# A transformer block on one core: the depthwise conv on TensorE in nine rounds instead of twelve, the Gram matrix in two column strips, and 79 instead of 71 bands convolved on TensorE

## The chip, the cores and the metric

One core of one Trainium2 chip runs the whole kernel. Its engines each work through their own queue in order: TensorE (matrix products), VectorE, ScalarE, GpSimd, and SyncE, which only issues DMAs. The metric is the device time in microseconds.

## The reference

The input x is 16 images of 128 channels, 96 x 96 pixels, f32. Cut to what matters:

```python
xn1 = layernorm(x over channels)
q, k, v = xn1 @ wq.T, xn1 @ wk.T, xn1 @ wv.T            # 8 heads of 16 channels
attn = softmax(l2norm(q) @ l2norm(k).T / 4)             # 16 x 16 per head, sums over all 9216 pixels
x = x + (attn @ v) @ wp.T
xn2 = layernorm(x over channels)
h1 = w_in @ xn2                                         # 128 -> 512 channels
h2 = depthwise 3x3 conv of h1, zero padding
x = x + w_out @ gelu(h2)                                # 512 -> 128 channels
```

## The kernel before

**What is tiled.** An image is worked on in 6 bands of 16 rows, so there are 96 bands (g from 0 to 95). The 512 hidden channels are four chunks of 128. A pair (band, chunk) that is convolved by VectorE is a "job". Pixels come in tiles of 128 (transposed to pixels x channels for the layer norm), four tiles to a call.

**First layer norm and attention.** Per four tiles: four transposes (`forth`, L716), statistics on VectorE (L723), a scaling by ScalarE (`scaled`, L759) into a buffer zT of four 128 x 128 tiles with a column of ones behind each, and a Gram product (`gram`, L768): per tile one product of the tile with itself and the column of ones, 129 columns, added up in one PSUM bank over the 72 tiles of an image. With the Gram matrix and the column sums, `attention` works out a 128 x 128 matrix per image in a chain of small steps; `mix` (L665) applies it. Transposes back to channels (`back`, L802) follow each norm, and ScalarE copies them (`place`, L805) into a ring of normalized rows, xn.

**The hidden layer on VectorE (`conv_job`).** `hidden` (L976): TensorE makes the 18 rows of h1 that a band and its halo need (or 16, with two rows copied over), ScalarE adds the bias (`kept`, L979). Of the nine taps, VectorE does six, one whole-band multiply-add each (`tap`, L1006); ScalarE scales two more (`product`, L999), which GpSimd's DMAs add (L1013); the weights are scaled such that the centre tap is one. `gelu` is L1017.

**The hidden layer on TensorE (`by_matmuls`).** Chunk 3 of some bands is not a job. `split` (L1083): for each of four groups k of 32 channels, four products of 128 x 32 put the left and right half rows and the even and odd rows into four strips of 32 partitions; so partitions 0 to 63 hold the left half (even rows, odd rows) and 64 to 127 the right half. The columns outside the image, and rows outside it, are filled with minus the bias by small products (L1085). ScalarE copies each group (`packed`, L1092). `conv`, called once for the even and once for the odd output rows (y): six taps t (two row offsets of the pair, three columns), two halves c, four groups k: 48 products, each 64 partitions (both row parities) by 32 channels, 384 columns. With 64 x 32 tiles, eight products (2 halves x 4 groups) lie side by side in the array; six such rounds make a call, twelve a band. A pair of row offsets covers four rows where three are needed; the fourth has weight zero. Two GELUs per call read the result (L1113).

**Output.** `ffn_out` (L1139) multiplies with w_out, ScalarE copies it out (`evicted`, L1149), a DMA adds it to the output.

**PSUM.** Two banks for the transposes `tr`, one for `bk`, one for the Gram matrix, and four "h" banks shared by hidden, split, conv, mix and out. A conv call holds two of them until its GELUs have read them.

**Which bands.** `by_pe(g)`: in the first image those in PE_FIRST, in the last those in PE_LAST, else a share PE_SHARE, 3 of 4: 71 bands. Where the kind of band changes to VectorE's, GpSimd sets the padding of chunk 3's buffer to zero (`around`).

**Order.** Each piece of work is entered in a plan with its engine, an estimated duration and a place (its due time, counted in jobs, plus the offset that the table AT holds for its kind). `Plan.order` simulates the engines with these durations: whenever an engine is free it starts the ready piece with the smallest place, if its buffers are free. The order of starts is the order of each engine's queue.

Of the kernel before, what the change touches and what calls it, by code (L numbers as in the profile page):

```python
# [18 lines left out]
BR = 16  # L19
# [3 lines left out]
PE_SHARE = [3, 4]  # L23
PE_LAST = [0, 1, 3, 4]
# [15 lines left out]
    load_1=-318.45, load_2=250.75, tables=-176.75, weights=-199.9, zeros=280.85, pads=489.4, pads_0=-50.0,  # L40
    load_a=-397.35, forth_a=-242.55, stats_a=-48.4, variance_a=52.55, power_a=346.4, scaled_a=65.85,
    gram=-109.85, back_a=-291.7, place_a=163.65, attention=-399.95, mix=-263.75, residual=-1.05, mixed=-9.75,
    add_x=163.65, forth_b=-248.0, stats_b=-54.25, variance_b=-72.2, power_b=-242.45, shift_b=-65.25,
    scaled_b=519.65, back_b=-664.1, place_b=430.4, evicted=-175.6, add_out=-299.05, halo=332.2, hidden=-67.95,
    kept=-6.5, products=623.75, add_last=230.4, tap=-40.35, add_first=521.3, gelu=615.7, split=-72.5,
    packed=65.05, conv=-64.0, conv_gelu=-632.25, out=-63.65, add=699.15, store=57.0, mix_0=-629.3,
    residual_0=-0.45, mixed_0=1.1, add_x_0=-191.4, gram_0=425.2, forth_a_0=-164.1, forth_b_0=-555.1,
    stats_a_0=-203.2, stats_b_0=31.65, scaled_a_0=166.35, scaled_b_0=435.1, back_a_0=198.1, back_b_0=63.05,
    place_a_0=213.65, place_b_0=-41.2, shift_b_0=-104.65, late=436.35, store_x2=-259.8, store_x2_0=-280.3,
    variance_a_0=296.05, variance_b_0=-572.0, power_a_0=446.6, power_b_0=-200.95, attention_0=-700.85,  # L50
    load_a_0=-699.6, hidden_0=-343.05, kept_0=688.75, products_0=-317.3, tap_0=406.55, add_last_0=-476.1,
    add_first_0=-25.55, gelu_0=-695.0, split_0=-310.35, packed_0=-61.1, conv_0=-522.45, conv_gelu_0=2.7,
    out_0=-354.3, evicted_0=38.2,
)
RESERVE = True
Q = 32
STEP = dict(scaled=1.089, hidden=0.115, products=-0.129, tap=-0.536, split=2.985, conv=0.6, out=0.866)
# [191 lines left out]
def tile_restormer_block(  # L249
# [68 lines left out]
    def column(t, v):  # L318
# [5 lines left out]
    whole = const.tile([P, 1], F32, name="whole")  # L324
    nbeta = const.tile([P, P], F32, name="nbeta")
# [20 lines left out]
    SW, SR = W // 2 + 2, BR // 2 + 1  # L346
    PART = SR * SW
    h1s = [
        h1p.tile([P, (BR + 2) * WP + 2 if n != PE_CHUNK else 4 * PART], F32, name=f"h1_{n}") for n in range(NCH)
# [4 lines left out]
    zT_bufs = [h1p.tile([P, QT, P + 1], F32, name=f"zT_{k}") for k in range(ZT_BUFS)]  # L354
# [36 lines left out]

    def at(kind, place, i=1):
        return place + AT[kind if i else kind + "_0"]
# [51 lines left out]
    def packed(k):  # L445
        return strips(h1s[PE_CHUNK][:, k * PART : (k + 1) * PART])

    def zeros(p):

        for t in zT_bufs:  # L450
            pool(300, at("zeros", p - 1), lambda t=t: nc.gpsimd.memset(t[:, :, P:], 1.0), [], [("w", "ones")])
        for t in h1s:
            pool(300, at("zeros", p), lambda t=t: around(t), [], [("w", "pads")])

    def weights(p):
# [8 lines left out]
        def loads_1():  # L464
# [7 lines left out]
            v["col"] = t[:, 10 * P + Q : 10 * P + Q + 24].rearrange("p (a t) -> p a t", a=2)  # L472
            v["by_part"] = t[:, 11 * P : 11 * P + 48]
            v["nb"] = t[:, 11 * P + 48 : 11 * P + 49]
# [78 lines left out]
        def column_of():  # L553
# [6 lines left out]
            nc.vector.tensor_scalar(v["nb"], b, -1.0, None, ALU.mult)  # L560
            nc.vector.tensor_reduce(whole, r, AX.X, ALU.add)
            nc.vector.tensor_scalar(whole, whole, b, None, ALU.mult)
            nc.vector.tensor_scalar(nbeta, ident, v["nb"], None, ALU.mult)
# [85 lines left out]
    def norm(i, second, place_of):  # L649
# [49 lines left out]
        def pixels(s, m):  # L699
# [80 lines left out]
            for h, (q, tr) in enumerate(zip(qs, trs)):  # L780
# [7 lines left out]
                if not second:  # L788
                    pe(QT * 219, at("gram", sh, i), lambda q=q: gram(q), [(*zt, 0), (*zt, 1), ("w", "ones")], [("g", i)])
# [458 lines left out]
```

## Time and profile before

| | before |
|---|---|
| median of 2 runs | 3908.46 us (3906.2 to 3910.72) |
| profiled execution | 3905.63 us, span 3903.9 us |
| granted TensorE clock, mean | 0.996 |
| busy: TensorE, VectorE, ScalarE, GpSimd | 3797.5, 3695.5, 3618.6, 1858.0 us |
| DMA: moved, mean rate | 790.94 MB, 203 GB/s |

How to read the profile: a group's row names the line, the engine, the operation, the tiles, the shape of the TensorE tile (rows*columns), partitions x elements, the count, then busy time and the mean of one in ns, then the idle time before it and what ended that. PE is TensorE's products, PEld its weight loads, DVE VectorE, ACT ScalarE, POOL GpSimd, SP SyncE. A product's length includes the way through the array, so that the lengths of consecutive products overlap; the distance from start to start says what one costs. In the slices each digit is the busy share of one fortieth of the span in tenths.

### The profile page before, as it was taken

How to read it: one execution, taken by the hardware profiler on the slowest of the kernel's cores; microseconds unless marked ns; L12 is line 12 of the kernel's file. 1: busy time of each engine (PE TensorE's matmuls, PEld its weight loads, DVE VectorE, ACT ScalarE, POOL GpSimd, SP SyncE). 2: the span in 40 equal slices, each digit the busy share in tenths (PEclk: the TensorE clock that was granted, in tenths of full speed). 3: DMA queues.
4: the chain of work that ended last, by engine and by line, in shares of the span. 5: the costliest groups of instructions: out<-in, count | busy, mean ns of one | idle time of the engine just before them, and what ended most of it. 6: DMA issues, size and time to landing. Idle time of an engine off the chain costs nothing.

```text
span 3903.9 us, 81207 instructions
## 1 busy us (share of the span) xinstructions
PE 3797.5 (97%) x32452; PEld 2337.7 (60%) x32452; DVE 3695.5 (95%) x3310; ACT 3618.6 (93%) x7473; POOL 1858.0 (48%) x1586
## 2 busy tenths in 40 slices
PE   8899999999999999999999999999999999999998
PEld 6556656566565665656556565665656656666544
DVE  6998999999999999999999999999999999999998
ACT  6899999999999999999999999999999999899995
POOL 4445555354454545545445454544545444454431
PEclk9999999999999999999999999999999999999999
DMA  5899999999999999999999999999999999999997
GB/s 145 174 200 224 193 211 210 200 223 190 218 201 203 221 191 222 196 206 218 186 214 202 208 217 190 224 199 211 216 184 223 203 213 206 195 221 192 205 186 161
DMA packets 188921, 790.94 MB, mean 203 GB/s; under 512 B 21888, under 2 KB 23424, under 8 KB 188544
## 3 DMA queue, kind: packets, MB, share of 16 engines
q0 software_dynamic: 130608, 633.92, 83.7%
q1 hardware_dynamic: 57936, 151.83, 10.8%
q8 instruction: 256, 4.19, 0.4%
q14 instruction: 121, 0.99, 0.1%
HBM read 150.62 MB, written 149.42 MB: 77 GB/s over the span
## 4 chain that ended last, share of the span: by engine, by line
PE 58%; ACT 15%; DMA 10%; DVE 9%; issue 4%; POOL 3%; POOLq 0%; ACTq 0%; DVEq 0%; SPq 0%
PE h L1139 15%; PE h L976 12%; PE h L1105 10%; DMA h<-h 8%; DVE h L1006 8%; PE h L665 4%; PE g L768 4%; ACT h L999 4%; PE h L1083 4%; ACT h L979 3%; ACT zT L759 3%; PE pB_b L802 2%; PE pT_b L716 2%; PE pB_a L802 2%; ACT h L1017 2%
## 5 line engine op out<-in xcount | busy, mean ns | idle before, releaser
L1006 DVE SCALAR_TENSOR_TENSOR h<-h,ratio,h 128x1520 f32<-128x1520 f32 (+1 forms) x1567 | 2750.3, 1779 | 13.7
L1013 POOL DMA_DIRECT2D h<-h x624 | 589.7, 964 | 1045.3 <-ACT h L999 416.6
L1139 PE MATMUL h<-h,woutT 128*128 128x384 f32 x3072 | 1059.6, 489 | 11.1 <-ACT h L979 7.0
L999 ACT ACTIVATE h<-h,ratio 128x1536 f32<-128x1536 f32 (+1 forms) x624 | 1012.4, 1638 | 2.4 <-DMA h<-h 1.3
L976 PE MATMUL h<-xn,winT 128*128 128x384 f32 (+3 forms) x2466 | 947.8, 500 | 31.5 <-ACT h L1149 13.2
L1139 PEld LDWEIGHTS h<-h,woutT 128*128 128x128 f32 x3072 | 570.7, 191 | 389.5 <-issue 21.2
L979 ACT ACTIVATE h<-h,beta 128x384 f32<-128x384 f32 (+1 forms) x1204 | 734.1, 659 | 26.4 <-PE h L976 19.8
L734 POOL TENSOR_TENSOR rstd_a<-ve_a,mhalf 128x4 f32<-128x4 f32 x288 | 545.0, 1895 | 360.3 <-ACT ve_a L730 347.6
L734 POOL TENSOR_TENSOR rstd_b<-ve_b,mhalf 128x4 f32<-128x4 f32 x288 | 528.9, 1841 | 345.6 <-ACT ve_b L730 334.2
L1006 DVE SCALAR_TENSOR_TENSOR h<-h,ratio 128x1536 f32<-128x1536 f32 x313 | 567.0, 1812 | 95.8 <-ACT h L979 94.7
L1105 PE MATMUL h<-h,taps 64*32 64x384 f32 x13632 | 584.7, 484 | 2.3 <-ACT h L979 2.3
L976 PEld LDWEIGHTS h<-xn,winT 128*128 128x128 f32 x2466 | 419.0, 190 | 232.6 <-ACT h L1149 26.6
L1017 ACT ACTIVATE h<-h 128x1536 f32<-128x1536 f32 (+1 forms) x316 | 484.5, 1534 | 32.6 <-DMA h<-h 31.8
L1105 PEld LDWEIGHTS h<-h,taps 64*32 64x32 f32 x13632 | 251.0, 106 | 288.5 <-issue 260.2
L759 ACT ACTIVATE zT<-pT_b,rstd_b 128x128 f32<-128x128 f32 x1132 | 338.0, 440 | 9.3 <-POOL rstd_b L734 8.4
L759 ACT ACTIVATE zT<-pT_a,rstd_a 128x128 f32<-128x128 f32 x1080 | 319.8, 421 | 18.1 <-POOL rstd_a L734 18.0
L768 PE MATMUL g<-zT 128*128 128x129 f32 x2160 | 286.8, 275 | 3.9 <-ACT zT L759 3.9
L665 PE MATMUL h<-xn,mwT 128*128 128x384 f32 x768 | 279.2, 490 | 3.2 <-ACT x L674 2.9
L768 PEld LDWEIGHTS g<-zT 128*128 128x128 f32 x2160 | 263.7, 191 | 6.7 <-ACT zT L759 4.3
L1149 ACT COPY h<-h 128x384 f32<-128x384 f32 x376 | 201.3, 535 | 60.9 <-PE h L1139 60.2
L1083 PE MATMUL h<-xn,winT 128*32 128x441 f32 (+4 forms) x2464 | 250.4, 507 | 1.7 <-ACT h L1113 1.7
L723 DVE BATCH_NORM_STATS2 st_b<-pT_b 128x6 f32<-128x256 f32 x566 | 211.9, 419 | 28.4 <-PE pT_b L716 19.3
(190 smaller groups left out, 3776.3 us busy)
## 6 DMA issues: line engine op xcount, KB each, us to landing
h<-h POOLq DMA_DIRECT2D x520, 768.0 KB, 9.5
h<-h POOLq DMA_DIRECT2D x104, 720.0 KB, 10.5
x<-in_x_dram SPq DMA_DIRECT2D x192, 384.0 KB, 7.5
out_dram<-x SPq DMA_DIRECT2D x190, 384.0 KB, 9.3
x<-in_x_dram POOLq DMA_DIRECT2D x189, 384.0 KB, 9.2
out_dram<-h POOLq DMA_DIRECT2D x94, 768.0 KB, 10.7
out_dram<-x SPq DMA_DIRECT2D x4, 192.0 KB, 1.9
h<-in_L_conv_w_in_dram SPq DMA_DIRECT2D x1, 256.0 KB, 2.7
```

The lines of the kernel that those rows point to most:

```text
L665: nc.tensor.matmul(rows(pm), lhsT=mats[i][0], rhs=interior(i, u), start=True, stop=True)
L734: nc.gpsimd.tensor_tensor(rstd, d["ve"], mhalf, ALU.pow)
L759: nc.scalar.activation(zT(q)[:, k, :P], d["pT", q][:, k, :], AF.Copy, scale=d["rstd"][:, t : t + 1])
L768: nc.tensor.matmul(grams[i][:, : P + 1], lhsT=zt[:, :P], rhs=zt, start=(q == 0 and k == 0), stop=(q == NU * TPU // QT - 1 and k == QT - 1),)
L976: nc.tensor.matmul(rows(ph)[:, k : k + m, :], lhsT=winT[:, n, :], rhs=z, start=True, stop=True)
L979: nc.scalar.activation(window(h1_, r, e - r, 1), rows(d.pop(("ph", r))), AF.Identity, bias=beta[:, n : n + 1])
L999: nc.scalar.activation(d["pr", t][:, o0:o1, :], shifted(t, o0, o1), AF.Copy, scale=ratio[:, n, t : t + 1])
L1006: nc.vector.scalar_tensor_tensor(h3[:, o0:o1, w0:w1], shifted(t, o0, o1, w0, w1), ratio[:, n, t : t + 1], onto, ALU.mult, ALU.add)
L1013: nc.gpsimd.dma_start(out=to[:, o0:o1, :], in_=d["pr", t][:, o0:o1, :], accum_op=ALU.add)
L1017: nc.scalar.activation(h3, h3, AF.Gelu)
L1105: nc.tensor.matmul(halves(d["pc", y, c][k * Q : (k + 1) * Q, :]), lhsT=taps[cs, k, 6 * y + t, :], rhs=packed(k)[cs, up : up + SR - 1, dx : ...
L1139: nc.tensor.matmul(rows(d["po"]), lhsT=woutT[:, n, :], rhs=h3s[g, n][:, s * UR : (s + 1) * UR, :], start=(k == 0), stop=(k == NCH - 1),)
```

## The change

- **Conv.** `conv(y)` is replaced by three steps. `both_rows(y)` does, for output rows of parity y, the three taps of the row pair of which both rows count: 24 products of 64 x 32, three rounds of eight. `single_rows` does the remaining row for both parities at once: for each column tap, half c, parity y and group k one product of 32 partitions (one half, one row parity) by 32 channels, 48 products, three rounds of sixteen 32 x 32 tiles, into all four result banks. The order is both_rows(0), single_rows, both_rows(1); the GELUs of the even rows follow the second step, those of the odd rows the third. Nine rounds instead of twelve, 96 products as before.
- **Packing.** Rows of the packed buffer now lie 50 elements apart with 49 of data; the element between two rows serves as the right neighbour of one and the left neighbour of the next. It is set by GpSimd (`sides`, four small products) whenever the kind of band changes to TensorE's, so the split's side columns are no longer products of each band. The split writes 441 columns per strip; only rows outside the image are still filled with small products.
- **Gram.** Each zT tile has a column of ones on both sides (130 columns). Two tiles k, k+1 are done together as four products of 128 x 64: of one tile, the left 64 channels against 129 columns and the right 64 against 65; of the other the reverse. The two column strips of the array get 194 columns each per pair of tiles. One product of zeros (one partition, 130 columns) opens the accumulation. The Gram matrix so has halves of its off-diagonal blocks in two places; `attention` copies it, transposes it on TensorE, and adds the two with two VectorE adds.
- **Bands.** PE_SHARE is 5 of 6 and PE_LAST has one more: 79 bands.
- **Plan.** Nearly all offsets in AT and STEP have other values, and the estimated durations of the changed pieces are lower (a Gram call 4 x 166 instead of 4 x 219 ns). The tables BY_BAND and BY_BLOCK, new, are empty.

```diff
-PE_SHARE = [3, 4]
-PE_LAST = [0, 1, 3, 4]
+PE_SHARE = [5, 6]
+PE_LAST = [0, 1, 2, 3, 4]
...
-    SW, SR = W // 2 + 2, BR // 2 + 1
-    PART = SR * SW
+    SW, SR = W // 2 + 1, BR // 2 + 1
+    PART = SR * (SW + 1) + 1
...
+    def sides():
+        for k in range(4):
+            nc.gpsimd.tensor_scalar(
+                h1s[PE_CHUNK][:, k * PART : (k + 1) * PART : SW + 1], ones_row[:, : SR + 1], npad[:, k : k + 1], None, ALU.mult
+            )
...
-                for k in range(QT):
-                    zt = zTs[q][:, k, :]
-                    nc.tensor.matmul(
-                        grams[i][:, : P + 1], lhsT=zt[:, :P], rhs=zt,
-                        start=(q == 0 and k == 0), stop=(q == NU * TPU // QT - 1 and k == QT - 1),
-                    )
+                    nc.tensor.matmul(grams[i][:, : P + 2], lhsT=ident[:1, :], rhs=ident[:1, 1:2].to_broadcast([1, P + 2]), start=True, stop=False)
+                done = q == NU * TPU // QT - 1
+                for k in range(0, QT, 2):
+                    for e, half in ((0, 0), (0, 1), (1, 1), (1, 0)):
+                        zt = zTs[q][:, k + e, :]
+                        c0, c1 = (0, P + 1 if e == 0 else P // 2 + 1) if half == 0 else (P // 2 + 1 if e == 0 else 1, P + 2)
+                        hs = slice(half * P // 2, (half + 1) * P // 2)
+                        nc.tensor.matmul(
+                            grams[i][hs, c0:c1], lhsT=zt[:, 1 + half * P // 2 : 1 + (half + 1) * P // 2], rhs=zt[:, c0:c1],
+                            start=False, stop=done and k + e == QT - 1,
+                        )
...
+        @step("PE", 110)
+        def _():
+            nc.tensor.transpose(ps([P, P], "ps_t"), v["gsb"], ident)
+
+        @step("DVE", 380)
+        def _():
+            for own, other in ((low, high), (high, low)):
+                to = v["gsb"][own, other]
+                nc.vector.tensor_add(to, v["ps_t"][own, other], to)
...
-        def conv(y):
-            for c in range(2):
-                d["pc", y, c] = bank((g, "conv", y, c), BR * W // 4)
-            for t in range(6):
-                up, dx = divmod(t, 3)
-                for c in range(2):
-                    cs = slice(c * 2 * Q, (c + 1) * 2 * Q)
-                    for k in range(4):
-                        nc.tensor.matmul(
-                            halves(d["pc", y, c][k * Q : (k + 1) * Q, :]),
-                            lhsT=taps[cs, k, 6 * y + t, :], rhs=packed(k)[cs, up : up + SR - 1, dx : dx + W // 2],
-                            start=(t == 0), stop=(t == 5),
-                        )
+        def product(y, c, k, up, dx, cs, first):
+            nc.tensor.matmul(
+                halves(d["pc", y, c][k * Q : (k + 1) * Q, :]),
+                lhsT=taps[cs, k, 6 * y + 3 * up + dx, :], rhs=packed(k, up, SR - 1, dx + c, W // 2)[cs],
+                start=first and dx == 0, stop=not first and dx == 2,
+            )
+
+        def both_rows(y):
+            if y == 0:
+                banks_of(0)
+            for dx in range(3):
+                for c in range(2):
+                    for k in range(4):
+                        product(y, c, k, y, dx, slice(c * 2 * Q, (c + 1) * 2 * Q), y == 0)
+
+        def single_rows():
+            banks_of(1)
+            for dx in range(3):
+                for c in range(2):
+                    for y in range(2):
+                        for k in range(4):
+                            q = 2 * c + y
+                            product(y, c, k, 1 - y, dx, slice(q * Q, (q + 1) * Q), y == 1)
...
+        steps = ((lambda: both_rows(0), pcs[0]), (single_rows, pcs[0] + pcs[1]), (lambda: both_rows(1), pcs[1]))
+        for z, (work, to) in enumerate(steps):
+            pz = p + STEP["conv"] * z
+            pe(3 * t_mm(UT) + 100, at("conv", pz, g >= HEAD), work, of, [*to, ("pk",), *h3])
+            for c in range(2 if z else 0):
+                act(t_act(UT, 1) - 43, at("conv_gelu", pz, g >= HEAD), lambda y=z - 1, c=c: gelu(y, c), [to[c]], h3)
```

More of the change, by code (lines that the diff above doesn't have):

```diff
@@ L39 @@
 AT = dict(
[L40 to L49, printed above, removed]
@@ new lines @@
+    gram=-63.6, back_a=-392.45, place_a=-178.95, attention=-393.35, mix=-544.9, residual=-1.05, mixed=92.45,
+    add_x=-573.6, forth_b=-240.05, stats_b=-110.6, variance_b=-283.15, power_b=-207.4, shift_b=-65.25,
+    scaled_b=435.55, back_b=-661.55, place_b=235.3, evicted=-205.85, add_out=-610.4, halo=160.95, hidden=-60.25,
+    kept=-144.95, products=700.0, add_last=-5.95, tap=663.25, add_first=-505.3, gelu=510.8, split=-292.15,
+    packed=-121.35, conv=-56.45, conv_gelu=137.85, out=-55.9, add=-373.95, store=-18.5, mix_0=-700.0,
@@ L54 @@
+    add_first_0=-60.5, gelu_0=-133.7, split_0=-148.25, packed_0=-73.9, conv_0=-162.05, conv_gelu_0=-182.8,
+    out_0=-279.1, evicted_0=566.9,
 )
 RESERVE = True
+CYCLE = 12
+BY_BAND = dict(
+)
+BY_BLOCK = dict(
+)
 Q = 32
-STEP = dict(scaled=1.089, hidden=0.115, products=-0.129, tap=-0.536, split=2.985, conv=0.6, out=0.866)
+STEP = dict(scaled=1.548, hidden=0.077, products=0.554, tap=-0.445, split=-0.184, conv=1.122, out=0.746)
 SLACK = dict(PE=450, DVE=120, ACT=130, POOL=410, ADD=200, MOVE=360)
@@ L390, in tile_restormer_block, with in_band @@
     op = plan.op
+    now = [0, 0]
     def at(kind, place, i=1):
-        return place + AT[kind if i else kind + "_0"]
+        kind = kind if i else kind + "_0"
+        own = BY_BAND[kind][now[0]] if kind in BY_BAND else 0.0
+        return place + AT[kind] + own + (BY_BLOCK[kind][now[1]] if kind in BY_BLOCK else 0.0)
+    def in_band(g, n=0):
+        now[:] = (NG - 1 - g) % CYCLE, n
     def h3_buf(key):
@@ L815, in norm @@
             for u in range(NU):
+                in_band(NB * i + u // UPB)
                 x2(place_of(u * TPU), u)
@@ L1208, in tile_restormer_block @@
                 whole_h1 = [("h1", PE_CHUNK, k) for k in ("first", "last", *range(7))]
-                if not by_pe(g):
-                    pool(300, at("pads", first[g], g >= HEAD), lambda: around(h1s[PE_CHUNK]), [], [*whole_h1, ("pk",)])
+                change = sides if by_pe(g) else lambda: around(h1s[PE_CHUNK])
+                pool(700 if by_pe(g) else 300, at("pads", first[g], g >= HEAD), change, [("w", "conv")], [*whole_h1, ("pk",)])
             for j, (g_, n) in enumerate(jobs):
                 if g_ == g:
+                    in_band(g, n)
                     conv_job(j, g, n)
+            in_band(g)
             if by_pe(g):
```

94 lines of the change are left out of this document (54 added, 40 removed).

## The prediction

> **What bounds the kernel now.** I read the page's head and slices first, then the waits of each engine, then the stretches.
>
> ```profile
> span 3903.9 us, 81207 instructions
> ...
> PE 3797.5 (97%) x32452; PEld 2337.7 (60%) x32452; DVE 3695.5 (95%) x3310; ACT 3618.6 (93%) x7473; POOL 1858.0 (48%) x1586
> ...
> PE   8899999999999999999999999999999999999998
> ...
> DMA  5899999999999999999999999999999999999997
> ```
>
> No stage stands out: TensorE is busy for 3797.5 of 3903.9 us, so it is idle for 106; VectorE is idle for 208, ScalarE for 285, and the DMA engines are at nine tenths or more from the third slice on. Who waits for whom (total, times, longest):
>
> ```profile
> PE pB_b L802 <- ACT xn L805: 17.0, 7, 4.7
> PE h L976 <- ACT h L1149: 13.2, 18, 1.8
> ...
> DVE h L1006 <- ACT h L979: 94.7, 46, 7.3
> DVE st_b L723 <- PE pT_b L716: 19.3, 19, 3.8
> ...
> ACT h L1149 <- PE h L1139: 60.2, 62, 3.3
> ACT h L1113 <- PE h L1105: 56.4, 31, 5.8
> ```
>
> TensorE's waits are small and scattered, while ScalarE's two largest are for TensorE (60.2 and 56.4). So TensorE comes first, VectorE and the DMA engines close behind it; a change pays only as far as it takes time from TensorE's queue and does not hand it to one of the others.
>
> **TensorE, step by step.** One stretch of its timeline (start, length, instructions merged) gives nearly every price. Each f32 product is two instructions here, two passes over the columns.
>
> ```profile
> 2025.51 0.60 PE L716 MATMUL pT_b<-ident,x 128*128 128x128 f32 x4
> 2025.95 1.06 PE L768 MATMUL g<-zT 128*128 128x129 f32 x8
> 2026.94 4.10 PE L1105 MATMUL h<-h,taps 64*32 64x384 f32 x96
> 2030.97 0.55 PE L802 MATMUL pB_b<-ident,zT 128*128 128x128 f32 x3
> 2031.36 0.81 PE L976 MATMUL h<-xn,winT 128*128 128x384 f32 x2
> ...
> 2032.44 1.06 PE L768 MATMUL g<-zT 128*128 128x129 f32 x8
> 2033.33 0.49 PE L802 MATMUL pB_a<-ident,zT 128*128 128x128 f32 x3
> 2033.66 1.46 PE L976 MATMUL h<-xn,winT 128*128 128x384 f32 x4
> ```
>
> From start to next start, a Gram call (L768) takes 0.89 us when another 128*128 product follows (2032.44 to 2033.33) and 0.99 when the conv's 64*32 products follow: changing the tile shape costs 0.09 to 0.10. The conv call takes 4.03. After it three transposes take 0.39 instead of 0.33: 0.06 more. The weight loads of the same call show its passes:
>
> ```profile
> 2027.29 0.15 PEld L1105 LDWEIGHTS h<-h,taps 64*32 64x32 f32 x8 [0.17 <-issue]
> 2027.61 0.15 PEld L1105 LDWEIGHTS h<-h,taps 64*32 64x32 f32 x8 [0.17 <-issue]
> ...
> 2030.19 0.15 PEld L1105 LDWEIGHTS h<-h,taps 64*32 64x32 f32 x8 [0.17 <-issue]
> ...
> L1105 PEld LDWEIGHTS h<-h,taps 64*32 64x32 f32 x13632 | 251.0, 106 | 288.5 <-issue 260.2
> ```
>
> Eight tiles per pass, a pass every 0.322 us (nine of them from 2027.29 to 2030.19), which is 0.84 ns per column; the eight loads, 106 ns each, fit in 0.15, so their starts lie some 6 to 7 ns apart. Twelve passes are 3.86, and 0.17 of the call is filling and draining. An excursion into another tile shape therefore costs 0.17 + 0.09 + 0.06 = 0.32 beyond its passes.
>
> *Conv.* 13632 weight loads at 192 a band are 71 bands: 142 calls of 12 passes, 142 x (3.86 + 0.32) = 594 us. The new form has three calls of six passes on 79 bands: 237 x (1.93 + 0.32) = 534, plus 79 x 0.05 for starting sixteen tiles rather than eight: 538. **-56 us**; at 71 bands it would be about -110. That sixteen 32x32 tiles run side by side no row shows. Below, I bound it by eight in 0.322 us (the single-row call then takes 12 passes: +153 us for 79 bands); above, by nothing lost. I take the side-by-side value, since the starts leave room: sixteen at 7 ns are 0.11 of 0.322.
>
> *Split.* The call now:
>
> ```profile
> 1661.45 0.95 PE L1083 MATMUL h<-xn,winT 128*32 128x441 f32 x8
> 1662.22 0.22 PE L1085 MATMUL h<-ones_row,nbeta 128*32 128x9 f32 x8
> 1662.28 0.93 PE L1083 MATMUL h<-xn,winT 128*32 128x441 f32 x8
> 1663.02 0.22 PE L1085 MATMUL h<-ones_row,nbeta 128*32 128x9 f32 x8
> 1663.17 0.55 PE L716 MATMUL pT_b<-ident,x 128*128 128x128 f32 x3
> ```
>
> 1.72 us for two k. Without the side columns 0.77 + 0.74 remain, and 0.09 of leaving: 1.60. With 0.15 for entry and reload, 142 x 1.87 = 266 becomes 158 x 1.75 = 277: **+11**.
>
> *Chunk 3 of eight bands* is no longer hidden by L976: 18 rows of 96, twice at 0.84 ns, are 2.9 us: **-23**.
>
> *Gram.* Per call each strip streams 2 x 2 x (129 + 65) columns, 0.65 us instead of 0.89, so by columns alone -69 for 288 calls. But every call becomes an excursion: 0.65 + 0.12 (fill and drain with less spread) + 0.15 = 0.92, **+9**. Neighbours that are themselves tiled share a change of shape, as the call at 2025.95 would, so -69 stays the lower end. A 64-column weight load is in no row (106 ns for 32 columns; 128-column loads, 128x129 passes, keep up with 0.11 each); if a 65-column pass took 0.11 like a 129-column one, the upper end is 288 x (0.86 + 0.27 - 0.89) = +69. I take +9, the nearer to the conv's own row. The sixteen one-row openings (two passes of 130 columns and a shape change, 0.32) and the attention's extra transposes (0.11) add **+7**.
>
> **The other engines**, from eight bands that leave VectorE:
>
> ```profile
> L1006 DVE SCALAR_TENSOR_TENSOR h<-h,ratio,h 128x1520 f32<-128x1520 f32 x1355 | 2402.0, 1793 | 12.2
> L1006 DVE SCALAR_TENSOR_TENSOR h<-h,ratio 128x1536 f32<-128x1536 f32 x313 | 567.0, 1812 | 95.8 <-ACT h L979 94.7 <-ACT ve_b L730 0.8
> L926 DVE TENSOR_TENSOR em<-e,blocks 128x128 f32<-128x128 f32 x16 | 4.5, 284 | 0.0
> ...
> L999 ACT ACTIVATE h<-h,ratio 128x1536 f32<-128x1536 f32 x520 | 850.6, 1651 | 2.1 <-DMA h<-h 1.3 <-DMA out_dram<-h 0.4
> L979 ACT ACTIVATE h<-h,beta 128x384 f32<-128x384 f32 x971 | 582.5, 650 | 16.8 <-PE h L976 14.5 <-DVE h L1006 0.5
> L1017 ACT ACTIVATE h<-h 128x1536 f32<-128x1536 f32 x312 | 482.8, 1547 | 32.2 <-DMA h<-h 31.8
> L1113 ACT ACTIVATE h<-h,whole 128x384 f32<-128x384 f32 x284 | 171.7, 612 | 56.6 <-PE h L1105 56.4
> L1092 ACT COPY h<-h 128x450 f32<-128x450 f32 x284 | 153.2, 596 | 2.3 <-DVE h L1006 2.0 <-PE h L1085 0.2
> ...
> q0 software_dynamic: 130608, 633.92, 83.7%
> ...
> h<-h POOLq DMA_DIRECT2D x520, 768.0 KB, 9.5
> ```
>
> VectorE: 8 x (1.812 + 5 x 1.793) = 86 less, 16 x 2 adds in the attention at about 0.3 (an estimate from the 284 ns of a 128x128 product) 10 more: -76. ScalarE: a VectorE band's chunk 3 costs 2 x 1.651 + 4 x 0.65 + 1.547 = 7.4, a TensorE band's 4 x (0.612 + 0.596) = 4.8: -21, and +3 for one more column copied per image. DMA: sixteen adds of 768 KB fewer, 12.6 of 633.92 MB, so 1.7% of the span, -65. GpSimd issues sixteen fewer and gains four small products per switch of the layout (by the rule in by_pe, 31 switches instead of 49); at 48% busy it hides them. Each switch must wait for the conv or the taps that read the old layout and now stands ahead of the packing when a TensorE band follows; behind it in GpSimd's queue are powers and DMA adds, which have slack by the same 48%.
>
> In the last stretch VectorE leads and TensorE waits:
>
> ```profile
> 3400.00:3800.00 400.00, 390.15 (x3237) 231.11 (x3241) 385.14 (x322) 376.64 (x757) 184.90 (x163) 1.00 0.98 203
> 3800.00:3904.00 104.00, 86.07 (x690) 43.75 (x678) 93.54 (x61) 59.12 (x79) 16.41 (x19) 0.95 0.77 159
> ```
>
> (busy TensorE, its loads, VectorE, ScalarE, GpSimd; clock; DMA share and rate). TensorE idles for 18 of these 104 us, against 2.5% before. The last image has one VectorE band fewer, 10.8 us; I count **-8** of it.
>
> **Sum.** -56 + 11 - 23 + 9 + 7 - 8 = -60. The profiled execution took 3905.6, 1.7 over its span; the median of the two runs shown is 2.8 above that. 3903.9 - 60 = 3844; with 4.5 it is 3848, rounded to 3850. Every other engine loses 18 to 76 us of work, so none overtakes TensorE: VectorE would be at 94%, ScalarE at 94%.
>
> **Rivals.**
>
> *VectorE and the DMA engines set the time* (0.25). If the Gram calls come beside other tiled calls or cost nothing beyond their columns, TensorE loses some 135 us and VectorE's -76 binds: 3832. If it also loses half of its direct waits for TensorE (19.3 in the row above; I put them all at 50), 3807; middle 3820. Against it: all 288 calls would have to find such neighbours.
>
> *The four h banks run out* (0.12). The single-row call opens the second pair of banks while the first is still held, so hidden, mix and out can't start until ScalarE has read two results, 2 x 0.612. One such stall per band is 79 x 1.2 = 95, half of it hidden 47: 3897 to 3945. For it: ScalarE is in order and 93% busy, and TensorE already waits for L1149's copies. Against: it can clear two banks during the following call.
>
> *Starts of the small matmuls bind* (0.05). A round of sixteen tiles has 32 starts in 0.644 us, 20 ns each. The rows bound the spacing by 7 ns, as inside a pass now, and by 42, a whole call over its starts (4.03 / 96). Midway, at 24.5 ns, a round takes 0.784: 79 x 3 x 0.14 = +33, 3883. The Trainium skill (TensorE: Matmul & The Clock Gate, section "Wait — 56ns, not 53.3ns?") gives a floor of about 25 ns from start to start, however small the matmul; by it this case is an estimate of +37. The eight starts within 0.05 above speak against such a floor between tiles.
>
> *Sixteen tiles don't run side by side* (0.06). The single-row call then lasts as long as twelve passes, +153: 4003, **slower** by 2.4%. It decides as soon as more than eight tiles can't stream at once; the forecast's -60 turns positive where the call takes 1.4 times its six passes. The same page (Part 3, "Measured speedup vs the span model") has sixteen tiles of 32x32 at 10.6 times one, which speaks against this; no run here shows it.
>
> **How the numbers follow.** The forecast has 0.50, its own range 3830 to 3880 (the Gram term and shared shape changes); the rest, 0.02, is unnamed. From 3810 to 3905 lies about 0.8: half of the VectorE case, the bank case's lower end and the issue floor are in it. Two per cent is about what a measurement of this kernel can tell from no change; 2% faster is below 3830.3, 2% slower above 3986.6. Faster by that: 0.17 of the VectorE case and 0.11 of the forecast's lower edge, 0.28; slower 0.07; within 0.65.
>
> **What would show it.** A TensorE idle share that stays near 106 us; conv calls near 2.1 us from start to next start, the 32*32 one no longer than the 64*32 ones; Gram calls near 0.77 and a longer first product behind each; L1085 gone but for the image's borders; VectorE near 3620. I am wrong if TensorE's busy share falls well under 96%, if the 32*32 call takes 4 us, or if L976 and L1139 begin to wait for L1113.

## The result, and the profile after

The changed kernel takes 4189.81 us (median of 2 runs, 4189.2 to 4190.41) against 3908.46: **7.2% slower**, ratio 1.0722 with an interval of 1.0704 to 1.0739. Forecast were 3850 us and a range from 3810 to 3905.

The head and slices of the changed kernel's page:

```profile
span 4187.2 us, 84643 instructions
...
PE 3886.8 (93%) x34240; PEld 2269.7 (54%) x34240; DVE 3646.4 (87%) x3296; ACT 3634.3 (87%) x7497; POOL 1898.2 (45%) x1616
...
PE   8889999999999999999999999999999999999978
...
DMA  5799799898898989989798997989989899897986
```

The span grew by 283 us. TensorE was to lose 60 us of work; its busy time *rose* by 89, and its idle time went from 106 to 300. No other engine took its place: all have lower shares than before. So every engine now waits more than before. One long stretch of both kernels, from the middle, shows that no single place does it (columns: stretch, length, busy TensorE, weight loads, VectorE, ScalarE, GpSimd, clock, DMA share, GB/s). The kernel before:

```profile
400.00:3400.00 3000.00, 2956.93 (x25627) 1826.43 (x25626) 2870.50 (x2523) 2838.79 (x5877) 1469.91 (x1208) 1.00 0.97 206
```

The changed kernel:

```profile
400.00:3400.00 3000.00, 2830.64 (x25422) 1653.57 (x25419) 2644.05 (x2342) 2663.42 (x5499) 1381.45 (x1152) 0.99 0.89 190
```

Of 3000 us TensorE idles for 169 instead of 43, and the DMA engines fell from 0.97 to 0.89. The changed kernel's largest waits of VectorE and ScalarE, and four of TensorE's (engine, line, waited for, total us, times, longest):

```profile
DVE h L1050 <- ACT h L1023: 297.7, 78, 7.3
...
ACT h L1170 <- PE h L1145: 65.7, 61, 4.0
...
PE h L1198 <- ACT h L1023: 43.6, 49, 1.5
...
PE h L1198 <- ACT h L1135: 38.7, 13, 3.8
...
PE h L1020 <- ACT h L1023: 34.3, 49, 1.8
...
PE h L1020 <- ACT h L1170: 14.8, 33, 2.1
```

(Lines have moved: L1050 is `tap`, L1023 `kept`, L1145 the conv's `product`, L1170 the TensorE bands' GELU, L1198 `ffn_out`, L1135 `packed`, L1208 `evicted`, L1020 `hidden`.) But for L1020 behind L1023, every TensorE row here is a product of one kind that waits until ScalarE has read a result of *another* kind: they share nothing but the h banks. The last row is a sign that the prediction had named for its being wrong, and the share of 93% is another. In the kernel before the same wait was this:

```profile
PE h L976 <- ACT h L1113: 6.0, 8, 0.8
```

VectorE's wait for `kept` tripled from 94.7 to 297.7. TensorE's timeline shows how one such chain hangs together:

```profile
2002.27 2.17 PE L1145 MATMUL h<-h,taps 64*32 64x384 f32 x48
2004.37 0.55 PE L829 MATMUL pB_b<-ident,zT 128*128 128x128 f32 x3
...
2006.11 1.56 PE L1020 MATMUL h<-xn,winT 128*128 128x384 f32 x4
...
2010.28 2.85 PE L1198 MATMUL h<-h,woutT 128*128 128x384 f32 x8 [0.55 <-ACT h L1023]
...
2014.31 0.90 PE L1145 MATMUL h<-h,taps 32*32 32x384 f32 x24
2015.42 2.56 PE L1145 MATMUL h<-h,taps 32*32 32x384 f32 x72 [0.20 <-ACT h L1208]
...
2019.40 2.17 PE L1145 MATMUL h<-h,taps 64*32 64x384 f32 x48
2021.50 3.21 PE L1126 MATMUL h<-xn,winT 128*32 128x49 f32 x48
2027.70 2.52 PE L1198 MATMUL h<-h,woutT 128*128 128x384 f32 x7 [2.99 <-ACT h L1135]
```

The three steps of one band start at 2002.27, 2014.31 and 2019.40. The first step's two banks stay occupied until ScalarE has read them with the GELUs behind the second step:

```profile
2017.25 1.05 ACT L1170 ACTIVATE h<-h,whole 128x384 f32<-128x384 f32 x2 [0.21 <-PE h L1145]
```

They end at 2018.30, so these banks are held for 16.0 us. Over all bands the median is 18.7 us, from a band's first conv product to the end of its second GELU; in the kernel before it is 6.2. Meanwhile hidden, mix, split and out share the other two. At 2014.31 the single-row step starts 24 of its 96 products and stops in the middle: one of its second pair of banks still holds an output that ScalarE evicts at that moment. At 2027.70 `ffn_out` waits 2.99 us for ScalarE's copies of the split, and these copies stood in ScalarE's queue behind a GELU that itself waited 3.08 us for a DMA:

```profile
2025.74 1.49 ACT L1061 ACTIVATE h<-h 128x1536 f32<-128x1536 f32 x1 [3.08 <-DMA h<-h]
2027.13 0.94 ACT L1135 COPY h<-h 128x441 f32<-128x441 f32 x2
```

That is a reading; what it costs is for the experiments.

### The profile page after: what moved, and what is told of

Read it like the earlier page. It is cut to its first block, busy times and chain, and to the rows that moved or that the text cites. A ratio compares the mean times of both kernels' runs of the same rounds, so it can differ in the third digit from the quotient of the medians.

```text
span 4187.2 us, 84643 instructions
## 1 busy us (share of the span) xinstructions
PE 3886.8 (93%) x34240; PEld 2269.7 (54%) x34240; DVE 3646.4 (87%) x3296; ACT 3634.3 (87%) x7497; POOL 1898.2 (45%) x1616
## 2 busy tenths in 40 slices
DMA packets 186631, 778.24 MB, mean 186 GB/s; under 512 B 21632, under 2 KB 23168, under 8 KB 186240
## 5 line engine op out<-in xcount | busy, mean ns | idle before, releaser
L1050 DVE SCALAR_TENSOR_TENSOR h<-h,ratio,h 128x1520 f32<-128x1520 f32 (+1 forms) x1527 | 2688.1, 1780 | 20.0
L1198 PE MATMUL h<-h,woutT 128*128 128x384 f32 x3072 | 1084.2, 497 | 84.5 <-ACT h L1023 43.6
L1020 PE MATMUL h<-xn,winT 128*128 128x384 f32 (+3 forms) x2398 | 944.1, 510 | 69.4 <-ACT h L1023 34.3
L1043 ACT ACTIVATE h<-h,ratio 128x1536 f32<-128x1536 f32 x608 | 971.8, 1611 | 29.6 <-DMA h<-h 23.8
L1198 PEld LDWEIGHTS h<-h,woutT 128*128 128x128 f32 x3072 | 574.4, 193 | 505.7 <-ACT h L1023 78.5
L1050 DVE SCALAR_TENSOR_TENSOR h<-h,ratio 128x1536 f32<-128x1536 f32 x305 | 553.1, 1813 | 316.6 <-ACT h L1023 297.7
L1023 ACT ACTIVATE h<-h,beta 128x384 f32<-128x384 f32 (+1 forms) x1172 | 684.8, 624 | 70.9 <-PE h L1020 57.2
L756 POOL TENSOR_TENSOR rstd_a<-ve_a,mhalf 128x4 f32<-128x4 f32 x288 | 491.1, 1707 | 409.8 <-ACT ve_a L752 362.9
L1145 PE MATMUL h<-h,taps 64*32 64x384 f32 (+1 forms) x15168 | 601.2, 494 | 17.6 <-ACT h L1023 9.1
L1020 PEld LDWEIGHTS h<-xn,winT 128*128 128x128 f32 x2398 | 411.9, 192 | 319.6 <-ACT h L1023 68.9
L1145 PEld LDWEIGHTS h<-h,taps 64*32 64x32 f32 (+1 forms) x15168 | 247.3, 105 | 301.4 <-issue 204.1
L696 ACT ACTIVATE x<-h,d 128x384 f32<-128x384 f32 x378 | 208.7, 603 | 43.3 <-DMA out_dram<-x 37.2
L1170 ACT ACTIVATE h<-h,whole 128x384 f32<-128x384 f32 x316 | 186.5, 619 | 67.2 <-PE h L1145 65.7
L832 ACT COPY xn<-pB_a 128x384 f32<-128x384 f32 x384 | 196.4, 511 | 53.9 <-PE pB_a L829 35.9
L795 PE MATMUL g<-zT 128*64 128x129 f32 x4320 | 240.8, 253 | 0.0
```

The costliest lines, as they stand in the source:

```text
L756: nc.gpsimd.tensor_tensor(rstd, d["ve"], mhalf, ALU.pow)
L1020: nc.tensor.matmul(rows(ph)[:, k : k + m, :], lhsT=winT[:, n, :], rhs=z, start=True, stop=True)
L1023: nc.scalar.activation(window(h1_, r, e - r, 1), rows(d.pop(("ph", r))), AF.Identity, bias=beta[:, n : n + 1])
L1043: nc.scalar.activation(d["pr", t][:, o0:o1, :], shifted(t, o0, o1), AF.Copy, scale=ratio[:, n, t : t + 1])
L1050: nc.vector.scalar_tensor_tensor(h3[:, o0:o1, w0:w1], shifted(t, o0, o1, w0, w1), ratio[:, n, t : t + 1], onto, ALU.mult, ALU.add)
L1145: nc.tensor.matmul(halves(d["pc", y, c][k * Q : (k + 1) * Q, :]), lhsT=taps[cs, k, 6 * y + 3 * up + dx, :], rhs=packed(k, up, SR - 1, dx + ...
```

## The experiments

The **theory** to start with: the order of the plan, which is written by offsets, no longer fits. The **rivals**: the operations cost more than forecast; the four banks run out; the share of bands; GpSimd's pads. Times without an interval are of a single run; the kernel before ranged from 3904 to 3914 us over all of its runs.

**1. Which half of the change?** Four kernels, one run each beside the kernel before (3913.89): the new operations with the old offsets, the same with the old bands, the old operations with the new offsets, and the changed kernel with durations in its plan as the trace has them.

```diff
 new_ops_old_offsets:     after, with the AT and STEP of before
 new_ops_old_offsets_71:  the same, and
-PE_SHARE = [5, 6]
+PE_SHARE = [3, 4]
 old_ops_new_offsets:     before, with the AT and STEP of after
 new_ops_true_durations:  after, with
-pe(QT * 166, at("gram", ...
+pe(QT * 240, at("gram", ...
-pe(2 * t_mm(SR * SW) + 150, at("split", ...
+pe(2 * t_mm(SR * SW) + 290, at("split", ...
-pe(3 * t_mm(UT) + 100, at("conv", ...
+pe(3 * t_mm(UT) + (1000 if z == 1 else 330), at("conv", ...
```

> The changed kernel with all operations and 79 bands, but the offsets AT and STEP of the kernel before. Theory 'offsets': the new table puts the pieces of the engines in an order that fits badly, so most of the 280 us comes back, under 4000 us. Theory 'banks': the single-row call needs all four h banks whatever the order, so it stays above 4080. Theory 'durations': the plan is misled by durations that are too short, with either table, so it stays within 60 us of 4190.

> The changed kernel's operations with the offsets AT, STEP and the 71 bands of the kernel before: the change of operations alone. Theory 'offsets': about 3850 to 3920. Theory 'banks': above 4050, with the 32x32 call still 3.2 us or more and the waits behind ScalarE. Theory 'durations': above 4050 too, but less if the true durations are given.

> The kernel before with its own operations and 71 bands, but with the offsets AT and STEP of the changed one. Theory 'offsets': 4050 or more, since the table alone spoils the order. Theories 'banks' and 'durations': within 60 us of 3908, since neither the four banks nor the mispriced pieces are in it.

> The changed kernel with nothing else changed but the durations that the plan reckons with: a Gram call 4 x 240 ns instead of 4 x 166, the conv steps 2.26, 2.93 and 2.26 us instead of 2.03, a split call 1.77 instead of 1.63, as the trace shows them with their changes of tile shape. Theory 'durations': under 4050 us, with TensorE's waits roughly halved. Theories 'offsets' and 'banks': within 60 us of 4190.

Measured: 4163.85, 4218.88, 4173.43 and 4265.22 us. So the share is not the cause (71 bands are slower still), and truer durations don't help: 75 us slower, which no theory expected. "Offsets" missed for the changed kernel itself: with the old table it should have come under 4000 us, and to 3850 to 3920 at 71 bands, but the new operations are slow with either set of offsets. What the third run shows is how much an order can cost: the old operations, none of them dearer, lose 260 us by other offsets alone. The head of this third run:

```profile
span 4171.7 us, 81163 instructions
...
PE 3908.3 (94%) x32452; PEld 2403.7 (58%) x32452; DVE 3719.9 (89%) x3310; ACT 3674.8 (88%) x7473; POOL 1785.3 (43%) x1586
```

The same 32452 products as before are busy for 3908 instead of 3797 us (at a granted clock of 0.967; see the last section), and TensorE idles for 263: the same picture as after, without any of its operations.

**2. How little disturbs the order?** The kernel before, with one offset of its table moved by 0.05 jobs, the smallest step in which its values are written.

```diff
 before_one_offset:
-forth_a=-242.55
+forth_a=-242.5
 before_other_offset:
-hidden=-67.95
+hidden=-67.9
```

> The kernel before with one of its 84 offsets moved by 0.05 job: forth_a from -242.55 to -242.5; no operation and no duration differs. Theory 'sharp order': the kernel before is fast only because its table fits its program to a hair, so this alone costs 100 us or more (about 4050). Theory 'operations': the order isn't what matters, so it stays within 30 us of 3914.

> As the last, but hidden from -67.95 to -67.9. Theory 'sharp order': 40 to 150 us slower, by another amount than the last. Theory 'operations': within 30 us of 3914.

Measured: 4033.62 and 3958.26 us beside 3908.14, so **+125 and +50**. Head of the first:

```profile
span 4031.9 us, 81332 instructions
...
PE 3851.5 (96%) x32452; PEld 2362.1 (59%) x32452; DVE 3693.5 (92%) x3310; ACT 3645.3 (90%) x7473; POOL 1798.9 (45%) x1586
```

An order that differs by next to nothing in its rule can cost twice what the whole change was to bring.

**3. The Gram matrix alone**, in the order of before, entry by entry (no piece added to the plan):

```diff
 before_gram_strips: before, and
-    nc.tensor.matmul(grams[i][:, : P + 1], lhsT=zt[:, :P], rhs=zt, ...)
+    ... four products of 128 x 64 a pair of tiles, opening and attention as in after
```

> The kernel before with the Gram product by halves in two column strips and the attention's extra copy, transpose and adds issued inside existing pieces; every entry of the plan, and so the order of all other work, is that of before. By the columns alone -69 us (3845); by the trace of the changed kernel (0.825 us to the next start plus 0.15 around it, 288 times, against 0.895) +24, so about 3938. Theory 'operations' would need 4000 or more here for its share of the loss; theory 'sharp order' says under 3970, since the order is kept.

Measured: 3946.13 us, ratio 1.0095 (1.0078 to 1.0112): **+38, where the prediction's terms were +9 and, for openings and attention, +7**. Its timeline:

```profile
2053.50 0.60 PE L716 MATMUL pT_a<-ident,x 128*128 128x128 f32 x4
2054.03 0.90 PE L773 MATMUL g<-zT 128*64 128x129 f32 x16
2054.86 0.55 PE L807 MATMUL pB_a<-ident,zT 128*128 128x128 f32 x3
2055.24 1.46 PE L987 MATMUL h<-xn,winT 128*128 128x384 f32 x4
```

The call takes 0.83 to the next start, the four transposes ahead of it 0.53 instead of 0.44, the three behind it 0.38 instead of 0.33: 0.97 against 0.89 before, times 288 is +23, if all calls are like this one. The openings and transposes of the attention were priced at +7; what the last 8 are was not followed.

**4. Why does the 32*32 call take 2.70 us?** In the changed kernel, loads and products of one that waits for nothing:

```profile
312.24 0.45 PEld L1145 LDWEIGHTS h<-h,taps 32*32 32x32 f32 x33 [0.17 <-issue]
312.91 1.40 PEld L1145 LDWEIGHTS h<-h,taps 32*32 32x32 f32 x63 [0.22 <-issue]
...
312.24 2.77 PE L1145 MATMUL h<-h,taps 32*32 32x384 f32 x96
314.94 0.55 PE L829 MATMUL pB_b<-ident,zT 128*128 128x128 f32 x3
```

33 loads run through, then none for 0.22 us. Sixteen tiles in two passes are 32 loads and 32 products. The theory to test: about 64 instructions can be under way at once, so the round behind must wait until the first has left. The test has twelve tiles in the same three rounds; the group of channels k = 3 is left out of the single-row step, so its hidden channels lack those taps.

```diff
 twelve_tiles: after, in product
-    start=first and dx == 0, stop=not first and dx == 2,
+    start=(first or k == 3) and dx == 0, stop=(not first or k == 3) and dx == 2,
 and in single_rows
-    for k in range(4):
+    for k in range(3):
```

> The changed kernel, but the single-row step leaves out the fourth group of channels, so that a round has 12 tiles of 32x32 and not 16. Theory 'queue of 64': sixteen tiles in two passes, each with its weight load, are 64 instructions a round, the next round can't be taken up until the first product of this one has left the array, and a call takes 2.70 us where it doesn't wait; with 48 a round it takes 2.1 (six passes of 0.322 and 0.17). Rival 'issue rate': the call is bound by starts some 17 ns apart, so 36 products take 2.70 x 36/48, that is 2.03, or, if the passes bind again, the same 2.1: then the loads of the second round tell it, one behind the other from the first round's end in that case, 0.05 to 0.1 us together in the first. The whole kernel stays above 4080 us.

The call took 2.49 us instead of 2.70; the theory had said 2.1, the rival 2.03 or 2.1 (time 4186.56 us):

```profile
3886.66 0.48 PEld L1145 LDWEIGHTS h<-h,taps 32*32 32x32 f32 x29 [0.17 <-issue]
3887.34 0.47 PEld L1145 LDWEIGHTS h<-h,taps 32*32 32x32 f32 x24 [0.19 <-issue]
3887.99 0.55 PEld L1145 LDWEIGHTS h<-h,taps 32*32 32x32 f32 x19 [0.17 <-issue]
...
3886.67 2.57 PE L1145 MATMUL h<-h,taps 32*32 32x384 f32 x72
3889.16 0.66 PE L738 MATMUL pT_b<-ident,x 128*128 128x128 f32 x4
```

Both missed, and the mechanism stays open. The first break now comes after 29 loads, the 24 of two passes and five of the next round, where it came after 33. The Trainium skill (TensorE: Matmul & The Clock Gate, Part 3, section "The mechanism") describes a window of 64 instructions within which loads are pulled ahead of products; 33 pairs of load and product fit that number, and 29 fit it only if pairs of the transposes ahead were still in the window, which the trace doesn't show. Against a plain count speaks that both breaks end at the same time, 0.67 and 0.68 us into the call. What is shown: sixteen tiles do run side by side, since the first sixteen products of the call at 312.24 start 6 to 7 ns apart, within 0.10 us, and last 0.5 us each; but three rounds of them in a row take 2.70 us and not 2.10.

**5. The four banks.** Two edits of the changed kernel that relieve them. One puts the conv back to two calls of six rounds, each with two banks of its own, so that TensorE has *more* to do: 79 x (2 x 4.03 - 2 x 2.10 - 2.70) is 92 us by the calls' prices. The other leaves every operation and lets the three steps of a band fall due together.

```diff
 old_conv_two_banks: after, with conv(0) and conv(1) as in before
 steps_at_once: after, with
-STEP = dict(... conv=1.122, ...)
+STEP = dict(... conv=0.0, ...)
 old_conv_two_banks_b, steps_at_once_b: the same with the AT and STEP of before
   (conv=0.6 there; 0.0 in the last)
```

> The changed kernel, its offsets, its 79 bands, its Gram strips and its packing, but the conv as before: two calls of twelve passes, each with its own two banks. TensorE has about 1.3 us more of conv work per band (8.1 against 6.8 us of calls that don't wait), some 100 us in all. Theory 'four banks': what costs most is that the single-row step opens the second pair of banks while the first is held, so that nothing else can be started; without it the kernel gets faster by 80 us or more, to 4000 to 4100, in spite of the added work. Theory 'sharp order' alone: another throw of an order that doesn't fit, 4150 to 4300. Theory 'durations': slower by the added work.

> The changed kernel with one number changed: STEP for the conv 0.0 instead of 1.122, so that the three steps of a band are due at the same time and follow each other closely, and the banks are held for a shorter time. Theory 'four banks': 60 us or more faster, 4130 or less, the 32x32 calls still 2.70 or more. Theory 'sharp order' alone: another throw, 4150 to 4300, either side of 4190.

Measured: 4041.55 and 4043.89 us, so **-148 and -146** against 4189.81. Heads, first the old conv:

```profile
PE 3902.7 (97%) x34240; PEld 2305.9 (57%) x34240; DVE 3633.5 (90%) x3296; ACT 3637.4 (90%) x7497; POOL 1844.7 (46%) x1616
```

and the steps at once:

```profile
PE 3846.1 (95%) x34240; PEld 2280.1 (56%) x34240; DVE 3646.5 (90%) x3296; ACT 3636.0 (90%) x7497; POOL 1779.0 (44%) x1616
```

With spans of 4039.8 and 4042.2 us TensorE idles for 137 and 196 instead of 300, in the first beside 16 us more busy time (not the 92 of the calls' prices; where the others went was not followed). VectorE's wait for `kept` falls to 111.0 and 101.8:

```profile
DVE h L1050 <- ACT h L1023: 111.0, 73, 5.6
```

```profile
DVE h L1050 <- ACT h L1023: 101.8, 70, 5.1
```

After experiment 2, any edit of the order might do this by luck. So both were repeated with the other set of offsets, where their partner took 4163.85:

> As old_conv_two_banks, but with the offsets of the kernel before, so a second throw of the order; its partner with the new conv is new_ops_old_offsets at 4164. Theory 'four banks': again 80 us or more faster than its partner in spite of the added TensorE work, under 4085. Theory 'sharp order' alone: the first gain was a lucky throw, now 4100 to 4260.

> As steps_at_once, but with the offsets of the kernel before (its STEP too, except the conv's, which is 0.0 and not 0.6). Partner: new_ops_old_offsets, 4164, where the steps are 0.6 of a job apart. Theory 'four banks': faster than its partner, by somewhat less than the 146 us of the first pair since the steps were nearer to each other there; under 4105. Theory 'sharp order' alone: 4100 to 4260, either side of the partner.

Measured: 4054.27 and 4072.26, **-110 and -92**. Four times of four the relief is 92 to 148 us, and all four relieved kernels (4042 to 4072) are faster than the changed kernel and the three of experiment 1 with its operations, in which the conv's steps stay apart (4164 to 4265). That it is the holding that changed, the traces show. From a band's first conv product to the end of its second GELU, the two banks of the even rows are held for 16.9 to 18.7 us (medians) in these last four, but for 7.2 and 6.6 with the old conv and 7.9 and 8.2 with the steps at once. Banks are not the only way to lose time, though: the old operations with the new offsets (experiment 1) hold them for 6.8 us and are 260 us slower than before.

**6. Split and pads.** The new packing in the kernel before, in its order, three times: with GpSimd's pads written ahead of the split, ahead of the packing, and there but on VectorE. In the first they are set so early that the VectorE band before overwrites them, so that part of its output differs.

```diff
 before_split_packing, _2, _3: before, with SW, SR, packed() and split as in after, and
+    sides()      # in _2 and _3 ahead of the first copy of the band (L1092)
 _3 only:
-    nc.gpsimd.tensor_scalar(
+    nc.vector.tensor_scalar(
```

> The kernel before with only the new packing and split: no side columns as products, 441 columns per strip, the pad elements set by GpSimd when the kind of band changes; 71 bands, old conv, old Gram, and the order of before entry by entry. By the step of the prediction, 0.12 us of each of 142 split calls: -17 us, 3891. At worst no change, if the split calls wait for something else anyway; it is the one part of the change that could beat the kernel before.

> As before_split_packing, but GpSimd sets the pad elements right before the first group of a band is packed and not before its split, so that GpSimd's queue isn't held up by taps that still read the old layout, and the VectorE band before it isn't disturbed. By the step of the prediction -17 us: 3891. Theory 'sharp order': the order is kept, but each split call ends earlier than the plan reckons; between 3880 and 3920.

> As before_split_packing_2, but the pads on VectorE. Theory 'GpSimd's pads': the 87 us that it lost go, and the -17 us of the split show: 3885 to 3915. Rival: the order of before doesn't bear a split call that ends earlier, 3950 or more.

Measured: 3950.4 (ratio 1.0114, 1.0097 to 1.0131), 3996.73 (1.0232, 1.0218 to 1.0246) and 3909.7 (1.0004, 0.9995 to 1.0013). The pads on GpSimd, and nothing else between the last two, cost 87 us. The row of the second, then of the third:

```profile
L452 POOL TENSOR_SCALAR h<-ones_row,npad 128x10 f32<-128x10 f32 x100 | 162.5, 1646 | 6.7 <-ACT ve_a L740 6.6
```

```profile
L452 DVE TENSOR_SCALAR h<-ones_row,npad 128x10 f32<-128x10 f32 x100 | 16.1, 238 | 0.9 <-ACT h L1009 0.9
```

The same hundred instructions take 1.65 us each on GpSimd and 0.24 on VectorE. Does that explain the changed kernel?

```diff
 sides_on_vector: after, in sides()
-    nc.gpsimd.tensor_scalar(
+    nc.vector.tensor_scalar(
```

> The changed kernel, every piece of the plan in the same order, but the four pad products per switch of layout are issued on VectorE, where they follow the taps anyway, and not on GpSimd. In the traces a GpSimd one takes 0.31 us or 3.4 to 3.5, 129 us for 64 in all, where the plan reckons 0.7 us for four, and ScalarE waits for GpSimd's powers behind them. Theory 'GpSimd's pads': 50 to 100 us faster, 4090 to 4140. Rival: GpSimd has the slack at 45% busy, within 30 us of 4190.

Hardly: 4179.61, 10 us less. In an order that waits elsewhere the pads cost little; that reading was not tested further by itself.

**7. All put together.** The new conv and packing with bands' steps due together, the old Gram matrix, durations as measured, and offsets searched anew; then the same with the pads on VectorE.

```diff
 new_conv_fitted: after, with the Gram matrix and attention of before, other values in AT, and
-STEP = dict(... conv=1.122, ...)
+STEP = dict(... conv=0.0, ...)
 new_conv_fitted_2: the same, in sides()
-    nc.gpsimd.tensor_scalar(
+    nc.vector.tensor_scalar(
```

> The changed kernel with 79 bands and the new conv in three steps due at the same time, but the Gram product and attention as before, the plan's durations as the traces show them, and offsets fitted anew to this program. Theory 'four banks and order': with the banks held shortly and a table that fits, the new conv comes out near the kernel before, 3860 to 3930. Rival 'operations': conv calls of 2.10, 2.70 and 2.10 us and 79 bands cost more than they save, whatever the order: above 3960.

> As new_conv_fitted, but the pads on VectorE. Theory 'GpSimd's pads': 50 us or more faster, 3960 or less, so that part of what was left is theirs. Rival 'operations': no more than 20 us.

Measured: 4010.06 (1.026, 1.0246 to 1.0274) and **3925.33** (1.0041, 1.0025 to 1.0056). Head of the last:

```profile
span 3926.1 us, 79874 instructions
...
PE 3801.2 (97%) x31888; PEld 2297.2 (59%) x31888; DVE 3642.9 (93%) x3328; ACT 3591.8 (91%) x7481; POOL 1793.2 (46%) x1552
```

TensorE idles for 125 us: nearly all of the loss is gone, with the new conv and 79 bands in place. 0.4% is left, and none of these versions beats the kernel before. How the pads reach the other engines is seen in ScalarE's wait for GpSimd's powers (`rstd`, the factors of `scaled`); first with the pads on GpSimd, then on VectorE:

```profile
ACT zT L780 <- POOL rstd_b L755: 76.3, 20, 11.3
```

```profile
ACT zT L780 <- POOL rstd_b L755: 4.5, 6, 1.1
```

In each of the 14 waits of the first kernel that are longer than 2 us the power stands right behind four pads in GpSimd's queue. The 72 us between the rows are near the 85 that the move brought.

## Why the prediction was wrong

**The step that failed** is the sum: it was taken as a change of TensorE's work, at an idle time that stays 106 us. The span came out 343 us above the 3844 of the forecast. 194 of them are idle time, which went from 106 to 300; 149 are busy time, which rose by 89 where it was to fall by 60. The idle time is no constant of the kernel. It is 180 when one offset of the kernel before is moved (experiment 2), and it falls from 300 to 137 and 196 when the conv's banks are held for a shorter time (experiment 5). The range made no allowance for this, though the diff gives nearly all offsets other values.

**The bank rival** came nearest, with 0.12 and 47 to 95 us. It was sized as one stall of TensorE per band, two GELUs long. Relief gave 92 to 148 us. The first two banks are held not for two GELUs but from the first step to the GELUs behind the second, 18.7 us in the median; and `hidden`, on which VectorE's taps hang, waits for the two that are left: VectorE's wait for `kept` fell from 297.7 to 111.0 and 101.8 with the relief. The view to read would have been the offset STEP["conv"] = 1.122 (in jobs) beside "into all four result banks". The other rivals fell: VectorE's share dropped; sixteen tiles do run side by side, and the call is 2.70 us rather than four; and the products of the first round start 6 to 7 ns apart, so that starts of 24.5 ns are not what binds there.

**The terms, one by one.**

- *Conv, -56*: the 64*32 call takes 2.10 (2002.27 to 2004.37), as said; the 32*32 call 2.70, not 2.1 plus 0.05. That is 0.55 x 79 = +43 of the 56, so the conv was to gain only 13. The rival on small starts (+33) was near in size, by another mechanism; what breaks the rounds stays open (experiment 4). And 2.70 is the price of a call that runs through: in the changed kernel only 30 of the 78 that stand alone in the trace do (no idle time of TensorE above 0.06 us in them), and the mean of all is 3.44.
- *Split, +11*: the call does get shorter, from 1.72 to 1.62 us in the median, 0.10 where the prediction's step was 0.12. But 142 such calls with the pads off GpSimd leave the time as it was (1.0004), so that these 15 us don't reach the time; the pads add 16 us to VectorE's work there. The share's part stays unmeasured alone.
- *Gram, +9*: +38 with openings and attention, where 9 + 7 stood. The call was to be 0.77 and is 0.83; the change of shape is 0.09 ahead and 0.05 behind, for 0.09 and 0.06.
- *GpSimd hides its four products*: it doesn't. They were costed at nothing because the engine was 48% busy; they cost 87 us in the kernel before, 85 in the fitted one, 10 in the changed kernel.
- *VectorE, -76*: 49 less in the profile (3646.4). *DMA*: 778.24 MB are moved, 12.70 less, where 12.6 was said. *Chunk 3, -23*, and *tail, -8*, were not measured alone.

How the 281 us divide depends on the order in which one takes the causes away. On the one path that was run, the steps at once bring 146; then the old Gram matrix, measured durations and searched offsets together 34; then the pads on VectorE 85; 17 are left. Taken singly, the pads cost 10 in the changed kernel, and the Gram matrix 38 in the kernel before, so the parts don't add up in any order. That the new table as such spoils the changed kernel is not shown, since the old one gives 4163.85. Offsets searched for the whole of the change, the Gram matrix included, were not run; nor was a version with more h banks.

The forecast of work alone was nearer than the total: in the last kernel TensorE is busy for 3801.2 us at 79 bands, where conv, split and chunk 3 were to bring -68 and brought +4. Of these 72, the 32*32 calls are 43, and the clock (below) is up to 31.

## What to carry to other kernels

In a kernel with three engines above 90% busy in an order worked out ahead, as here, idle time is a property of the order: before pricing a change by its instructions, ask whether the order is still the one that was fitted, and give the range what a small shift of it costs here, 50 to 125 us. Count buffers by how long they are held, from the first instruction that opens them to the last reader, not by how many there are; a step that needs all of them waits until the last one is free, and what it holds keeps the others out. And "hidden, since that engine is half idle" wants a check of what the next engine waits for: a small operation can delay what stands behind it in the queue although the engine has time.

## What the hardware showed that was not expected

**Short waits close together lower the granted clock.** The view by cores of the changed kernel, whose clock was 0.996 before:

```profile
core 0: 4187.2 us, clock 0.982
```

(1 - 0.996) x 3904 is 16 us of lost clock, (1 - 0.982) x 4187 is 75. So up to 60 us of TensorE's longer busy time are the clock's; in the last kernel (0.988) it is up to 31. The trace records the granted clock as steps, and only two values occur, 1.00 and 0.50. The stretches at 0.50 last 3.41 us or a multiple of it, but for one that the kernel's end cuts off: 7 of them, 34 us together, in the kernel before, and 25, 153 us together, in the changed one. In the 3.41 us ahead of 24 of these 25, TensorE had been busy for at most 0.55 of the time. One such pair of stretches, the second at half clock (columns as in the long stretch above):

```profile
1588.84:1592.26 3.42, 1.59 (x10) 0.74 (x9) 3.42 (x5) 2.34 (x4) 0.86 (x1) 1.00 1.08 208
1592.26:1595.67 3.41, 3.41 (x68) 1.65 (x70) 3.41 (x4) 0.21 (x1) 3.11 (x2) 0.50 1.10 230
```

TensorE idles for 1.83 of the first 3.42 us, and no single wait there is longer than 1.02. The Trainium skill (TensorE: Matmul & The Clock Gate, Part 1, section "What's actually happening") halves the clock after an idle window of some 3.4 us; the length agrees with this trace, but here a window that was idle for about half of it was enough.

**A small GpSimd operation beside VectorE's taps.** Of the changed kernel's 64 pad products of 128x10, 31 take 0.31 to 0.33 us and 31 take 3.35 to 3.51 (the other two 2.10 and 16.5). One of each kind, and what VectorE did meanwhile:

```profile
874.74 0.33 POOL L464 TENSOR_SCALAR h<-ones_row,npad 128x10 f32<-128x10 f32 x1 [0.75 <-DVE h L1050]
875.34 3.50 POOL L464 TENSOR_SCALAR h<-ones_row,npad 128x10 f32<-128x10 f32 x1
```

```profile
874.54 0.76 DVE L745 BATCH_NORM_STATS2 st_a<-pT_a 128x6 f32<-128x256 f32 x2
875.21 1.79 DVE L1050 SCALAR_TENSOR_TENSOR h<-h,ratio,h 128x1520 f32<-128x1520 f32 x1
876.92 1.81 DVE L1050 SCALAR_TENSOR_TENSOR h<-h,ratio 128x1536 f32<-128x1536 f32 x1
```

The short one runs beside the statistics; the long one starts beside a tap and ends at 878.84, 0.11 us after the end of the next tap. All 33 that are not short end 0.11 to 0.20 us after the end of a VectorE instruction. The Trainium skill (SBUF — State Buffer, section "SBUF: two separate sides") says that VectorE and GpSimd share a pair of ports as an exclusive lock, which a VectorE instruction with two inputs in SBUF holds to its end against a GpSimd instruction that reads SBUF. The ends in this trace agree with that, and on VectorE the same product takes 0.24 us (experiment 6); no run made the taps of one input to prove it.

**Rounds of 32*32 tiles**: the sixteen products of a first round start within 0.10 us, but three rounds in a row take 2.70 us where the 64*32 calls take 2.10 (experiment 4); why is open.
